# Three graph layers, regrouped: consecutive-node tiles, two column blocks, and an order written by hand

## The chip, the cores and the metric

The kernel runs on one core of a Trainium2 chip. The metric is the device time of one execution in microseconds (us); lower is better. The median of three runs before the change is 11253.15 us.

## The reference, cut to what matters

The graph has N = 3327 nodes with 128 features, and a dense-stored adjacency `adj` of 3327 x 3327 (fp32). Four layers each normalise `x`, apply a ReLU and add the layer's result to `x`:

```python
h = relu(layernorm(x)); x = x + L0(h, adj)   # 128 x 8-dim attention, softmax over N; ends in out @ Wo.T
h = relu(layernorm(x)); x = x + L1(h, adj)   # hyperbolic: h @ embed, scale per node, adj @ y, concat @ layer
h = relu(layernorm(x)); x = x + L2(h, adj)   # h @ weight.T, scale per node, adj @ xt, scale per node, relu
h = relu(layernorm(x)); x = x + L3(h, adj)   # (A/deg) @ h @ W_in + (A.T/deg_T) @ h @ W_out
```

The scalings per node of layers 1 and 2 are long chains on one number per node (norm, sqrt, tanh, artanh, division). So after layer 0 there are four products of an adjacency with a node matrix: `adj @ y` in layer 1, in layer 2, and in layer 3 once with `adj` and once with its transpose.

## The kernel before, in words

Layer 0 (lines 1 to about 800) is a hand-ordered attention that fills the first 10290 us; its instructions are the same, in the same order on every engine, before and after the change. It leaves its unnormalised heads in DRAM (`oT_d`, 8 rows and a row of sums) and a transposed adjacency `adjT`.

What follows runs in nine stretches, and a scheduler sets the order of their instructions:

- **Output projection** (loop at L876 to L891). For each pair of node tiles, `ot` is loaded from `oT_d` (1152 KB, L876), divided by its sums on DVE (`rc`, reciprocal, L878; product, L879), transposed on PE (L886), copied by ACT or DVE (`evac`, L132 and L136), multiplied with `woT` (L890) and added to `xs` (L891). A node tile `t` holds the nodes p*26+t, one per partition p.
- **Before product 1.** `layer_norm` (L922, L923, L927), transposes and sums of squares (`transposed_squares`, L957, L942, L946: squares on ACT, summed on PE with a vector of ones), a projection (`project`, L969) whose result DVE copies (L1044), sums of squares by rows (`row_squares`, L976, L977), and then the chain of small operations: class `Small` (L158 to L191) makes one 128 x 26 result per operation, on DVE, with `sqrt`, `tanh` and `Ln` on ACT (L185). Last, ACT and DVE write `y` (L1058, L981).
- **Product 1** (`aggregate`, L992 to L997). For each of 26 source tiles a strip of 128 rows x 3327 columns of `adjT` is loaded, from SP's and POOL's queue in turn, into one of four buffers. PE multiplies it with `y[:, t, :]` in seven column chunks of up to 494, which accumulate in seven PSUM banks. DVE sums each strip's rows (`degT`, L997) for layer 3.
- **Between products 1 and 2, 2 and 3**: the results leave PSUM through `by_tiles`, which reorders columns to the tiles, and the same kinds of steps follow for all 26 tiles at once.
- **Products 2, 3 and 4.** Product 3 reads `adj` itself, product 4 `adjT`; there is no work between 3 and 4 but the copies, and product 4 carries the projection of product 3's result beside it (`also`).
- **End.** `add_projected` (L1147) per four tiles, and stores of `out` from SP's and POOL's queue (L1166, L1169).

Nothing of a product starts before the steps in front of it are done for all nodes, since every product needs all of `y` as its sources. PE, DVE and ACT each run their instructions strictly in the order given.

Of the kernel before, what the change touches and what calls it, by code (L numbers as in the profile page):

```python
# [67 lines left out]
def rows_of(t):  # L68
    return P - 1 if t == NT - 1 else P
# [22 lines left out]
def gnn_kernel(ctx: ExitStack, tc: tile.TileContext, x, adj, Wq, Wk, Wv, Wo, embed, layer,  # L92
# [709 lines left out]

    wts = ctx.enter_context(tc.tile_pool(name="wts", bufs=1))
    xs = load_x(wts)
    ones = wts.tile([P, 1], F32, name="ones")
    nc.vector.memset(ones, 1.0)

    def on_all(v, name):
        o = wts.tile([P, D], F32, name=name)
        nc.sync.dma_start(o, v.unsqueeze(0).to_broadcast([P, D]))  # L810
        return o
# [15 lines left out]
    def clip_of(sm, n):  # L827

        return sm.ts(sm.recip(n), L2_MAXNORM, ALU.mult, 1.0, ALU.min)

    eb, lb, hb = on_all(embed_bias, "eb"), on_all(layer_bias, "lb"), on_all(bias, "hb")
    eb2, lb2, b2 = row_sum("eb2", eb), row_sum("lb2", lb), row_sum("b2", hb)
    with tc.tile_pool(name="w0", bufs=1) as w0:
        sm = Small(w0, "s")
        b2w = sm.new()
        nc.vector.tensor_copy(b2w, b2.to_broadcast([P, NT]))
        bn = sm.ts(sm.sqrt(b2w), L2_MIN_NORM, ALU.max)
        bt = sm.act(bn, AF.Tanh)
        bc = sm.mul(sm.div(bt, bn), clip_of(sm, sm.ts(bt, L2_MIN_NORM, ALU.max)))
        nc.vector.tensor_scalar(hb, hb, bc[:, 0:1], None, op0=ALU.mult)  # L840
    hb2 = row_sum("hb2", hb)
    emb_w = wts.tile([P, D + 1], F32, name="emb_w")
    nc.sync.dma_start(emb_w[:, 0:D], embed)
    lay_w = [wts.tile([P, D + 1], F32, name=f"lay_w{i}") for i in range(2)]
    for i in range(2):
        nc.sync.dma_start(lay_w[i][:, 0:D], layer[i * P:(i + 1) * P])
        with_product(lay_w[i], lb)
    with_product(emb_w, eb)
    w_in = wts.tile([P, D], F32, name="w_in")
    nc.sync.dma_start(w_in, W_in)  # L850
    w_out = wts.tile([P, D], F32, name="w_out")
    nc.sync.dma_start(w_out, W_out)
    w2T = wts.tile([P, D + 1], F32, name="w2T")

    degT = wts.tile([P, NT], F32, name="degT")
    nc.vector.memset(degT, 1.0)
    with tc.tile_pool(name="f1", bufs=1) as f1, tc.tile_pool(name="f2", bufs=4) as f2, \
            tc.tile_pool(name="f_ps", bufs=3, space=PSUM) as f_ps:
        w_raw = f1.tile([P, D], F32, name="w_raw")
        nc.sync.dma_start(w_raw, weight)  # L860
        ps = f_ps.tile([P, 4, P], F32, name="ps_t")
        nc.tensor.transpose(ps[:, 0, :], w_raw, ident)
        nc.vector.tensor_copy(w2T[:, 0:D], ps[:, 0, :])
        with_product(w2T, hb)
        wo = f1.tile([P, HD], F32, name="wo")
        nc.sync.dma_start(wo, Wo)
        wo_e = wo.rearrange("o (i e) -> o e i", e=H)
        woT = f1.tile([P, H, P], F32, name="woT")
        for k0 in (0, 4):
            ps = f_ps.tile([P, 4, P], F32, name="ps_t")  # L870
            for i in range(4):
                nc.tensor.transpose(ps[:, i, :], wo_e[:, k0 + i, :], ident)
            evac(woT[:, k0:k0 + 4, :], ps)
        for t0 in range(0, NT, 2):
            ot = f2.tile([P, H + 1, 2 * P], F32, name="ot")
            (nc.sync if t0 % 4 else nc.gpsimd).dma_start(ot, places(oT_d, t0, 2, H + 1))  # L876
            rc = f2.tile([P, 2 * P], F32, name="rc")
            nc.vector.reciprocal(rc, ot[:, H, :])  # L878
            nc.vector.tensor_tensor(ot[:, 0:H, :], ot[:, 0:H, :], rc.unsqueeze(1).to_broadcast([P, H, 2 * P]),  # L879
                                    op=ALU.mult)  # L880
            for i in range(2):
                oT = f2.tile([P, H, P], F32, name="oT")
                for k0 in (0, 4):
                    ps = f_ps.tile([P, 4, P], F32, name="ps_t")
                    for e in range(4):
                        nc.tensor.transpose(ps[:, e, :], ot[:, k0 + e, i * P:(i + 1) * P], ident)  # L886
                    evac(oT[:, k0:k0 + 4, :], ps)
                py = f_ps.tile([P, D], F32, name="ps_y")
                for e in range(H):
                    nc.tensor.matmul(py, oT[:, e, :], woT[:, e, :], start=(e == 0), stop=(e == H - 1))  # L890
                nc.vector.tensor_tensor(xs[:, t0 + i, :], xs[:, t0 + i, :], py, op=ALU.add)  # L891

    big = ctx.enter_context(tc.tile_pool(name="big", bufs=1))
    strips = ctx.enter_context(tc.tile_pool(name="strips", bufs=4))
    part = ctx.enter_context(tc.tile_pool(name="part", bufs=3))
    banks_u = ctx.enter_context(tc.tile_pool(name="banks_u", bufs=1, space=PSUM))  # L900

    def bank_u(i):
        return banks_u.tile([P, 4 * P], F32, name=f"pu{i}")

    turn = [0]

    def next_bank():
        turn[0] += 1
        return bank_u(turn[0] % 7)

    def arr(name, w=D):
        return big.tile([P, NT, w], F32, name=name)

    def matT(name):
        return big.tile([P, NP], F32, name=name)

    def layer_norm(sm, xs, h):

        mv = sm.pool.tile([P, NT, 2], F32, name="mv")
        for t in range(NT):  # L920
            st = part.tile([P, 6], F32, name="st", bufs=8)
            nc.vector.bn_stats(st, xs[:, t, :])  # L922
            nc.vector.bn_aggr(mv[:, t, :], st)  # L923
        r = sm.recip(sm.sqrt(sm.ts(mv[:, :, 1], LN_EPS, ALU.add)))
        off = sm.mul(sm.ts(mv[:, :, 0], -1.0, ALU.mult), r)
        for t in range(NT):
            nc.scalar.activation(h[:, t, :], xs[:, t, :], AF.Relu, scale=r[:, t:t + 1], bias=off[:, t:t + 1])  # L927

    def columns_of(c):
        ts = tiles_of(c)  # L930
        return slice(ts[0] * P, (ts[-1] + 1) * P)

    def column_squares(sm, of, dst_of=None):


        o = sm.new()
        ps = bank_u(7)
        for c in range(7):
            ts = tiles_of(c)
            src = of(c)  # L940
            sq = part.tile([P, 4 * P], F32, name="sq")
            nc.scalar.activation(sq[:, :len(ts) * P], src, AF.Square)  # L942
            if dst_of is not None:
                nc.vector.tensor_copy(dst_of(c), src)
            for t in ts:
                nc.tensor.matmul(ps[:, t:t + 1], sq[:, (t - ts[0]) * P:(t - ts[0] + 1) * P], ones,  # L946
                                 start=True, stop=True)
        nc.vector.tensor_copy(o, ps[:, :NT])
        return o

    def transposed_squares(sm, h, hT):

        def of(c):
            ps = next_bank()
            ts = tiles_of(c)
            for t in ts:
                nc.tensor.transpose(ps[:, (t - ts[0]) * P:(t - ts[0] + 1) * P], h[:, t, :], ident)  # L957
            return ps[:, :len(ts) * P]
        return column_squares(sm, of, lambda c: hT[:, columns_of(c)])

    def project(lhsT, w, take):

        k = w.shape[-1]
        step = 4 * P // k
        for t0 in range(0, NT, step):
            ts = range(t0, min(t0 + step, NT))
            ps = next_bank()
            for t in ts:
                nc.tensor.matmul(ps[:, (t - t0) * k:(t - t0 + 1) * k], lhsT[:, t * P:(t + 1) * P], w,  # L969
                                 start=True, stop=True)  # L970
            take(ts, ps[:, :len(ts) * k].rearrange("p (t o) -> p t o", o=k))

    def row_squares(dst, ts, rows):

        sq = part.tile([P, 4, P], F32, name="sq")
        nc.scalar.activation(sq[:, :len(ts), :], rows, AF.Square)  # L976
        nc.vector.tensor_reduce(dst[:, ts[0]:ts[-1] + 1], sq[:, :len(ts), :], axis=AX.X, op=ALU.add)  # L977

    def add_scaled(dst, a, s, b):

        nc.vector.scalar_tensor_tensor(dst, a, s, b, op0=ALU.mult, op1=ALU.add)  # L981

    def aggregate(y, strip_of, deg=None, also=None):


        width = [min(AW, N - c * AW) for c in range(7)]
        pu = [bank_u(c) for c in range(7)]
        for t in range(NT):
            m = rows_of(t)
            s = strips.tile([P, N], F32, name="strip")  # L990
            for p0, p1 in pieces(m):
                (nc.sync if t % 2 else nc.gpsimd).dma_start(s[p0:p1], strip_of(t, p0, p1))  # L992
# [208 lines left out]
```

## Time and profile before

| | us |
|---|---|
| median of three runs | 11253.15 |
| lowest, highest | 11250.1, 11254.57 |
| the profiled execution | 11256.11 |
| its span, first to last instruction | 11254.3 |
| the part behind layer 0 (from 10290.3) | 964.0 |

Busy shares over the whole span are PE 96%, ACT 90%, DVE 76%, but these are the shares of the attention. A row of the windows view gives the length of a stretch, then each engine's busy time with its number of instructions, then PE's granted clock as a fraction, the DMA engines' busy share and GB/s.

### The profile page before, as it was taken

To read this page: it belongs to the slowest core of one execution; us is meant where nothing else is said; L and a number is where in the kernel's file an instruction comes from. 1 tells how busy PE (TensorE), PEld (TensorE's weight loads), DVE (VectorE), ACT (ScalarE), POOL (GpSimd) and SP (SyncE) were. 2 spreads that over 40 slices of the span, in tenths; PEclk is the share of its full clock that TensorE was granted. 3 is DMA by queue.
4 is the path that set the end of the run, shared out by engine and by line. 5 is a ranking of instruction groups with operands and counts; after the bars stand their busy time and mean duration, and the time that the engine had idled before them with its cause. 6 is when DMAs were issued, how large, how long until landed. Compare 5 with 4: busy or idle time off the path is not lost. (4 is left out here: it accounts for less than half of the span.)

```text
span 11254.3 us, 205118 instructions
## 1 busy us (share of the span) xinstructions
PE 10750.9 (96%) x72980; PEld 3640.0 (32%) x72980; DVE 8537.9 (76%) x13563; ACT 10117.6 (90%) x13718; POOL 1974.8 (18%) x3079
## 2 busy tenths in 40 slices
PE   4599999999999999999999999999999999998779
PEld 2233333333333333333333333333333333334444
DVE  5588887888878887788887888878887777777533
ACT  3599999999999999999999999999999999996210
POOL 5111211111111111111111111111111111111000
PEclk8799999999999999999999999999999999999889
DMA  8855555555555554555555555555554545454457
GB/s 245 252 91 94 96 89 111 91 94 96 89 111 91 96 93 80 111 89 97 93 91 111 90 97 93 92 111 89 96 91 82 108 79 85 78 87 118 158 183 272
DMA packets 652680, 1243.35 MB, mean 110 GB/s; under 512 B 185966, under 2 KB 527990, under 8 KB 635148
## 3 DMA queue, kind: packets, MB, share of 16 engines
q1 hardware_dynamic: 609768, 1100.61, 50.4%
q0 software_dynamic: 41888, 129.51, 3.9%
q8 instruction: 591, 9.68, 0.4%
q14 instruction: 433, 3.55, 0.1%
HBM read 1082.90 MB, written 146.60 MB: 109 GB/s over the span
## 5 line engine op out<-in xcount | busy, mean ns | idle before, releaser
L659 ACT ACTIVATE e<-S 128x952 f32<-128x952 f32 (+1 forms) x9408 | 8697.9, 1146 | 14.5 <-PE S L647 11.4
L700 PE MATMUL po<-e,VA 128*9 128x476 f32 (+1 forms) x46592 | 5736.2, 564 | 20.2 <-DVE OS L708 1.1
L640 DVE TENSOR_TENSOR S<-a,shb 128x476 f32<-128x476 f32 (+1 forms) x5824 | 4037.5, 693 | 1760.9 <-ACT e L659 1299.5
L647 PE MATMUL S<-QS,KT 64*128 64x476 f32 (+1 forms) x23296 | 4843.4, 447 | 54.5 <-DVE S L640 45.8
L647 PEld LDWEIGHTS S<-QS,KT 64*128 64x128 f32 x23296 | 2410.3, 184 | 5143.4 <-ACT e L659 1465.8
L662 ACT ACTIVATE e<-S 128x476 f32<-128x476 f32 (+1 forms) x3808 | 2358.7, 758 | 2.4 <-PE S L647 2.1
L682 DVE SCALAR_TENSOR_TENSOR e<-e,h 128x476 f32<-128x476 f32 (+1 forms) x2016 | 1389.9, 689 | 46.2
L712 POOL DMA_DIRECT2D oT_d<-OS x896 | 470.7, 531 | 4791.2 <-DVE OS L708 4707.5
L566 POOL TENSOR_SCALAR QS<-QS 32x476 fp32r<-32x476 f32 (+1 forms) x1344 | 982.9, 731 | 1453.6 <-DMA QS<-qS_d 801.1
L700 PEld LDWEIGHTS po<-e,VA 128*9 128x9 f32 x46592 | 692.7, 88 | 1608.5 <-issue 1514.3
L673 DVE TENSOR_SCALAR h<-S 128x476 f32<-128x476 f32 (+1 forms) x672 | 439.0, 653 | 77.6 <-PE S L647 4.9
L677 DVE TENSOR_TENSOR h<-h,h 128x476 f32<-128x476 f32 (+1 forms) x672 | 443.1, 659 | 0.0
L684 DVE SCALAR_TENSOR_TENSOR e<-e,h 128x476 f32<-128x476 f32 (+1 forms) x672 | 440.8, 656 | 0.0
L682 DVE SCALAR_TENSOR_TENSOR e<-h 128x476 f32<-128x476 f32 (+1 forms) x672 | 438.3, 652 | 0.0
L576 POOL COPY VA<-VR 128x832 f32<-128x832 f32 x224 | 225.5, 1007 | 972.0 <-DMA VR<-v_d 733.8
L132 ACT COPY uT<-pu 128x494 f32<-128x494 f32 (+1 forms) x12 | 6.6, 547 | 428.2 <-PE pu L994 428.2
L675 DVE TENSOR_SCALAR h<-h 128x476 f32<-128x476 f32 (+1 forms) x672 | 323.4, 481 | 23.2
L994 PE MATMUL pu<-strip,h 128*128 128x494 f32 (+2 forms) x728 | 294.6, 566 | 38.9 <-ACT h L927 38.9
L994 PE MATMUL pu<-strip,y 128*128 128x494 f32 (+2 forms) x728 | 296.5, 570 | 29.3 <-DVE y L981 18.3
L679 DVE TENSOR_SCALAR h<-h 128x476 int32<-128x476 f32 (+1 forms) x672 | 279.3, 416 | 23.0
L291 DVE STREAM_TRANSPOSE cols<-rows 128x416 f32<-128x416 f32 x208 | 204.1, 986 | 21.8 <-DMA rows<-in_adj_dram 14.2
L994 PEld LDWEIGHTS pu<-strip,h 128*128 128x128 f32 (+1 forms) x728 | 138.5, 191 | 191.2 <-issue 141.8
(184 smaller groups left out, 2319.0 us busy)
## 6 DMA issues: line engine op xcount, KB each, us to landing
KT<-kS_d SPq DMA_DIRECT2D x1792, 208.0 KB
KT<-kS_d SPq DMA_DIRECT2D x1792, 104.0 KB
VR<-v_d SPq DMA_DIRECT2D x224, 416.0 KB
strip<-adjT POOLq DMA_DIRECT2D x39, 1663.5 KB, 7.7
strip<-adjT SPq DMA_DIRECT2D x36, 1663.5 KB
QS<-qS_d SPq DMA_DIRECT2D x3072, 14.9 KB
QS<-qS_d SPq DMA_DIRECT2D x1536, 29.8 KB
adjT<-cols SPq DMA_DIRECT2D x26, 1664.0 KB
```

What stands on the lines that cost most here:

```text
L566: nc.gpsimd.tensor_scalar(QS[b][r0:r0 + 32, j + 1, :w], QS[b][r0:r0 + 32, j, :w].bitcast(F32), -1.0, 0.0, op0=ALU.mult, op1=ALU.add)
L640: touch(u, [r], nc.vector.tensor_tensor(bank(u, r), adj_of[c][2 * q + r][:, :w], shift_of[c][:, :w], op=ALU.subtract))
L647: x = nc.tensor.matmul(bank(u, r), KT[b][64 * r:64 * r + 64, max(0, j - 1), q * P:(q + 1) * P], QS[b][64 * r:64 * r + 64, j, :w], start=Fa ...
L659: touch(u, (0, 1), nc.scalar.activation(e[:, :, :w], S[:, odd:even + 1, :w], AF.Exp, scale=2.0))
L662: touch(u, [r], nc.scalar.activation(e[:, 1 - r, :w], bank(u, r), AF.Exp, scale=2.0))
L673: touch(u, [1], nc.vector.tensor_scalar(f, bank(u, 1), LOG2_E2, EXP_LEAST, op0=ALU.mult, op1=ALU.max))
L677: nc.vector.tensor_tensor(f, f, whole, op=ALU.subtract)
L682: nc.vector.scalar_tensor_tensor(e, f if k == 4 else e, EXP_C[k], f, op0=ALU.add, op1=ALU.mult)
L684: nc.vector.scalar_tensor_tensor(e, e, EXP_C[0], power.bitcast(F32), op0=ALU.add, op1=ALU.mult)
L700: nc.tensor.matmul(po[32 * j:32 * j + H + 1, :w], VA[k % 2][:, 2 * pairs[v][2] + of, j, :], e_of[v, j][:, 1 - of, :w], start=(q == 0 and r ...
L712: nc.gpsimd.dma_start(oT_d[:, d * N + c * CW:d * N + c * CW + w], o[32 * j:32 * j + H + 1, :w])
L994: nc.tensor.matmul(pu[c][:, :w], y[:m, t, :], s[:m, c * AW:c * AW + w], start=(t == 0), stop=(t == NT - 1))
```

## The change

Everything behind layer 0 is rewritten; what is computed stays the same. The parts:

- A node tile now holds 128 consecutive nodes. `x`, `out`, `oT_d` and the strips are read and written in that layout: 512-byte runs for `x`, `out` and `oT_d`, consecutive rows for the strips. Results leave PSUM in plain column order (`copied`), without `by_tiles`.
- The 26 tiles are two blocks, `BLOCKS = (range(0, 16), range(16, 26))`. Each product is made in two column blocks of 2048 and 1279 columns (four and three PSUM banks of up to 512 columns); product 4 in three, of 1791, 1024 and 512. A strip is one block's columns of 128 rows: 234 strips instead of 104, in six buffers.
- The steps before and behind a product run per block, as Python generators (`pre1`, `post1`, `pre2`, `post2`, `pre3`), each step followed by a `yield` of the us that it is taken to last. `aggregate` calls `tick` after every matmul, which issues the next steps when their time has come; `drain` issues all that is left. A scheduler no longer moves anything (`manual_schedule`).
- The second block's `y` is waited for only at source tile 16 (`drain(ready)`).
- The projection of layer 0 goes tile by tile, with loads four tiles ahead (`f_load`, `f_norm`, `f_turn`, `f_mul`), and block 0's `pre1` starts beside its last ten tiles.
- Squares of `h` are summed by rows on ACT and DVE (`squared`), no longer on PE; the degrees are summed per block (four `deg` vectors).

```diff
+    BLOCKS = (range(0, 16), range(16, NT))
-    strips = ctx.enter_context(tc.tile_pool(name="strips", bufs=4))
+    strips = ctx.enter_context(tc.tile_pool(name="strips", bufs=6))
+    ctx.enter_context(tc.manual_schedule())
...
+    def tick(us):
+        while chains and us > 0:
+            c = chains[0]
+            if c[1] > us:
+                c[1] -= us
+                return
+            us -= c[1]
+            try:
+                c[1] = next(c[0])
+            except StopIteration:
+                chains.popleft()
+
+    def drain(until=None):
+        while chains and (until is None or until in chains):
+            for _ in chains.popleft()[0]:
+                pass
...
+    def feed(k):
+        while strip_list and len(strip_held) < k:
+            rows, t, c0, w = strip_list.popleft()
+            s = strips.tile([P, 4 * 4 * P], F32, name="strip")
+            for p0, p1 in pieces(rows_of(t)):
+                (nc.sync if t % 2 else nc.gpsimd).dma_start(s[p0:p1, :w], rows[t * P + p0:t * P + p1, c0:c0 + w])
+            strip_held.append(s)
...
+        for t in range(NT):
+            if ready is not None and t == second[0]:
+                drain(ready)
+            feed(6)
+            m = rows_of(t)
+            s = strip_held.popleft()
+            for c in cs:
+                k = width(c)
+                nc.tensor.matmul(got[c][:, :k], y[:m, t, :], s[:m, c * 4 * P - c0:c * 4 * P - c0 + k],
+                                 start=(t == 0), stop=(t == NT - 1))
+                tick(k * 0.00172)
+            if deg is not None:
+                nc.vector.tensor_reduce(deg[:m, t:t + 1], s[:m, :deg_w or w], axis=AX.X, op=ALU.add)
...
+    use(7, 4, 5, 6)
+    ready = start(pre1(1))
+    start(keep1(0))
+    start(keep1(1))
+    got = aggregate(ys[0], first, 0, ready=ready, deg=deg[0], deg_w=final[0][0] * P)
+    drain()
+    use(7, 0, 1, 2, 3)
+    start(both(post1, pre2, 0, got))
+    got = aggregate(ys[0], second, 4)
+    drain()
+    use(7, 4, 5, 6)
+    ready = start(both(post1, pre2, 1, got))
+    got = aggregate(ys[1], first, 0, ready=ready)
+    use(7, 0, 1, 2, 3)
+    start(both(post2, pre3, 0, got))
+    got = aggregate(ys[1], second, 4)
+    drain()
```

`keep1` is the projection with the first half of `layer`; `use` names the PSUM banks left to the steps; `both` runs one block's `post` and the next layer's `pre`.

## The prediction

> **What bounds the kernel now.** I read the stretches behind layer 0 first (windows view): the change leaves the first 10290 us instruction for instruction as they are.
>
> ```profile
> 10290.30:10330.00 39.70, 2.46 (x10) 1.79 (x10) 20.42 (x38) 3.60 (x5) 5.25 (x8) 0.54 0.98 324
> 10330.00:10413.50 83.50, 76.50 (x624) 72.30 (x624) 76.20 (x124) 16.50 (x27) 5.04 (x5) 0.96 0.46 147
> 10413.50:10472.30 58.80, 37.75 (x183) 31.66 (x183) 32.64 (x126) 28.14 (x62) 0.00 (x0) 0.64 0.00 1
> 10472.30:10621.00 148.70, 148.00 (x364) 69.89 (x364) 89.01 (x51) 8.99 (x28) 6.94 (x13) 0.98 0.80 286
> 10621.00:10730.90 109.90, 49.40 (x235) 43.17 (x235) 67.09 (x315) 44.12 (x85) 0.00 (x0) 0.56 0.05 18
> 10730.90:10880.00 149.10, 148.41 (x364) 70.04 (x364) 9.41 (x29) 9.02 (x28) 6.86 (x13) 0.98 0.80 286
> 10880.00:10939.60 59.60, 14.31 (x78) 13.99 (x78) 45.28 (x158) 16.23 (x27) 0.00 (x0) 0.56 0.08 29
> 10939.60:11239.00 299.40, 299.21 (x780) 144.86 (x780) 92.08 (x60) 13.63 (x33) 12.69 (x24) 0.99 0.76 273
> 11239.00:11254.30 15.30, 6.07 (x52) 5.88 (x52) 7.01 (x27) 0.30 (x1) 7.14 (x14) 0.82 0.36 113
> ```
>
> Columns: stretch, length, then busy us of PE, PEld, DVE, ACT, POOL, then clock, DMA share, GB/s. The four products (rows 4, 6, 8) are PE-bound. Between them lie 58.8 + 109.9 + 59.6 = 228.3 us in which no product runs, and 123.2 us of projection. PE's waits say what is late there:
>
> ```profile
> PE pu L957 <- ACT h L927: 48.4, 2, 40.3
> PE pu L994 <- ACT h L927: 38.9, 1, 38.9
> PE ps_t L862 <- DMA ot<-oT_d: 34.7, 1, 34.7
> PE pu L994 <- DVE y L981: 18.3, 1, 18.3
> PE ps_t L886 <- ACT oT L132: 4.5, 13, 0.7
> ```
>
> The reader is to see the per-node chains on DVE and ACT, and a first load. The price of a product comes from two finer windows:
>
> ```profile
> 10472.30:10476.30 4.00, 4.00 (x5) 1.79 (x6) 0.50 0.00 0
> 10476.30:10480.30 4.00, 4.00 (x10) 1.82 (x9) 0.86 0.00 0
> 10500.00:10600.00 100.00, 100.00 (x252) 47.54 (x251) 1.00 0.84 305
> ```
>
> At full clock, 252 half-products in 100 us at 475 columns on average: 1.67 ns a column, 144.5 us for 26 x 3327. A start after an idle PE runs at clock 0.50 and 0.86 first: about 3 us lost.
>
> **The change part by part.** Block pieces of a product cost 26 x columns x 1.67 ns: 88.9 us (2048), 55.5 (1279), 77.8 (1791), 44.5 (1024), 22.2 (512). PE work of the steps now lies beside them at the full-clock price of its rows: 0.27 us a tile for a 129-wide projection (L969), 0.24 for a sum with ones (L946), 0.17 for a transpose (L957). Counts are from the changed kernel's own order of instructions.
>
> *Projection of layer 0* (123.2 us now). In front of tile 2's load SP issues Wo, tile 0 and all of `x`; POOL issues two tiles and nine small loads. That is 5.1 MB, at the first row's 324 GB/s 16 us, so tile 2 is there at about 10310. Then 24 tiles at 2.9 us (before: 5.8 us from one pair's L890 to the next), 6 us for the last tile's division, transposes and products: 10386. DVE has 0.87 + 1.14 + 0.27 = 2.3 us of its own a tile (half of L878 and L879, and L891) and gets some 19 us of preparation and layer norm in bursts, of which its 0.6 us a tile hide a part; I take 14: 10400, or 110 us. The loads are 30,000 packets of 512 bytes. Such packets moved at 289 GB/s (the loads of Wq and Wk at 11 to 13 us), so 17 MB take 59 us and the first strips 14 more, under PE's pace; if latency uncovers them it costs up to 20. Bounds 98 to 133.
>
> *Before product 1* (58.8 now): layer norm's statistics and ReLU lie under the last tiles. What is left for block 0: 4.6 us of ReLU and squares, 23 small operations 9 (with `Ln`'s table), first copies 1, six projections 6.5 at ACT's 1.04 us a group (copy and square 0.5 each), then 52 small operations, which take 11.9 us now (10460.4 to 10472.3): 34.
>
> *Product 1, first piece.* 88.9 + PE work 11.4 + a cold start 3. DVE issues in order: `y` of block 0 (5 us), statistics, degree sums of 1.65 us (L997's 3.62 for 3327 columns, by width), 23 small operations, so the first copy of `hT` is done near 28 us and the third near 31, while PE comes to the projection at 23: 10 us of stall with the ReLU before it. The 52 operations in one burst hold up the degree sums and with them the strips' buffers: strip 11 lands near 58 us, wanted at 53: 4.5. Together 118.
>
> *Product 1, second piece, with `post1` and `pre2` of block 0.* PE needs 55.5 + 8. The chain: sums and projection 26 us (paced by PE), 46 small operations 12, `xs` 32 x 0.263 = 8.4, statistics 4.2, small 3.4, ReLU 16 x 0.39 = 6.2, squares 2.5, small 8.5, copies and projection 8.5, and 60 small 14.7 (10716.2 to 10730.9 now): 94.5. Uncovered: 95.5 - 63.5 = 32.
>
> *Product 2, first piece.* The same chain with 10 tiles in front of source tile 16: PE first waits 4 us for ACT's squares behind block 0's `y`; then 19 to the end of the projection, 12, 5.3, 2.6, 3.4, 3.9, 2, 8.5, PE's projection at 64 to 69, and 60 small operations and a first `y`, 15.5: `y` of tile 16 at about 86 us. PE is there at 70. Then 34.2 and a cold start 3: 123.
>
> *Other pieces.* `post2` and `pre3` of block 0 need 43 us and have 62.5 (55.5 + 6.5 and a copy): hidden. For block 1 they need 52 and have 60: hidden, 88.9 + 4 + 2 = 95. Their cover gone, they would cost those 43 and 52. Then 55.5, 78, 54.5 (44.5 and 40 tiles of 0.22, L1147, under 1.2 us a group), 26 (with 2 for loads of 256 KB each, for which PE takes 0.85 us).
>
> *End* (15.3 now): one four-tile group instead of seven, one store instead of 21 issues: 9.
>
> *Strips:* 243 issues instead of 108 at POOL's 0.53 us, alternately on two queues, against 0.85 us or more of PE time each; the rate needed is the same or lower (250 GB/s over these pieces, now 305). Nothing.
>
> *Waits.* PE gets some 69 groups of step work between its products, each behind ACT or DVE. Where such a result just arrives, PE waited 4.5/13 = 0.35 us. Bounds 0 and 24; most have slack by the prices above, so 6. Behind each such wait stand the rest of the piece on PE, then the strips' buffers, and on SP and POOL the loads of the next strips; nothing else is queued there until the stores of the end.
>
> Sum: 110 + 34 + 118 + 95.5 + 123 + 62.5 + 95 + 55.5 + 78 + 54.5 + 26 + 9 + 6 = 867, now 964.0: 97 us less. The span 11254.3 becomes 11157.3; the median of the runs lies 1.15 below this span: **11156**.
>
> Splitting doubles the per-node chains: 583 small operations and 50 table loads instead of 301 and 24. A table load takes 1.283 us in the trace, and the `sqrt` behind it starts 0.02 us later (10319.23 behind 10317.93 + 1.28), with 0.14 us between DVE's result and the load. The Trainium skill ("ScalarE: Activation LUTs", What ACT_TABLE_LOAD costs) counts a further drain of about 1.38 us for each switch, 2.66 in all. By the row the sum stands; with the page's drain on the 29 loads of the uncovered chains an estimate would be 40 us more, 11196. The trace shows no such drain, so it stays out of the sum.
>
> **The rivals.** *A, the guesses of the order are short, PE waits often* (14%). For: the `yield` of a ReLU is 0.28 us against the row's 0.39, and bursts are counted at 0.3 or 0.5 of their length. Against: most steps end on DVE and ACT, which run ahead of PE. All 69 waits at 0.35 (+18) and four stalls of 5 us with a cold start of 3 (+32): 11206.
>
> *B, more is hidden* (14%). For: DVE is 40% idle in product 1 and nearly free in product 2; my chains add stages end to end. If a third of 32 + 16 + 14.5 + 34 is gone: -32, 11124.
>
> *C, the cover fails: slower* (4%). One engine order; if the chains of the blocks ran with the products stopped, as PE's waits on `y` would do if the order were wrong, all per-block chains would be paid: 34 + 60 + 94.5 + 85 + 43 + 52 = 368 against the 110 that I leave uncovered (34 + 17.5 + 32 + 19 + some 7): 258 more, 11414. It decides for slower from 97 us, that is when less than 161 of the 258 us are covered. Against: the operands of the first piece's sources 0 to 15 do not depend on block 1.
>
> *D, the change does not do what it says* (2%): if the first piece waited for all 26 tiles of `y` and not for block 0, the gaps would stay as they are; projection and end save 13 + 6: 11234.
>
> *E, a table switch costs about twice its row* (2%): another 1.283 us on each of the 29 switches of the uncovered chains is 37: 11193. Against: the 0.02 and 0.14 us above. (The Trainium skill's drain, cited there, is of this size.)
>
> **How the numbers follow.** My forecast 65%, A 14%, B 13%, C 4%, D 2%, E 2%. Its own range, from the projection (-12, +23), the waits (-6, +18) and 15 us either way in the two long chains: 11128 to 11190. To leave out no more than 2 in 10 with B and A: 11118 to 11210. A measurement of this kernel tells 0.2% (22 us) from no change. Faster by more: my forecast, A, B and E, 94%; within: D, 2%; slower: C, 4%.
>
> **What would show it.** In the profile of the changed kernel: product pieces at clock 1.00 and 1.67 ns a column; PE waiting on DVE `y` once before product 2 (about 25 us) and once in its first piece (about 16); in product 1's first piece stalls on the copy of `hT` and on a strip; none in layer 3; end of the projection near 10400. I am wrong if PE waits on strips all along, if layer 2 to 3 shows a gap, or if the projection takes over 133 us.

## The result, and the profile after

| | before | after |
|---|---|---|
| median of the runs, us | 11252.85 (11250.1 to 11254.57, 4 runs) | **11114.46** (11112.16 to 11115.49, 4 runs) |
| span of the profiled execution | 11254.3 | 11113.3 |
| end of layer 0 (its last product on PE) | 10290.2 | 10284.7 |
| the part behind it | 964.1 | 828.6 |

The ratio is 0.9877, with a 95% interval of 0.986 to 0.9894: 138.4 us less. The prediction said 97 less, 11156, in a range from 11118 to 11210; the time lies 3.5 us below that range. The direction was right; the predicted saving was 41 us too small.

Windows view of the changed kernel, one row per stage of the prediction's sum (stretch, length, busy us of PE, PEld, DVE, ACT, POOL, clock, DMA share, GB/s):

```profile
10284.70:10398.20 113.50, 83.28 (x639) 80.28 (x636) 75.31 (x152) 38.08 (x69) 21.30 (x29) 0.85 0.69 208
10398.20:10429.50 31.30, 9.01 (x48) 7.27 (x47) 20.93 (x92) 18.44 (x39) 0.63 (x2) 0.70 0.09 34
10429.50:10531.20 101.70, 101.19 (x291) 49.51 (x292) 72.33 (x164) 30.54 (x71) 6.87 (x13) 0.98 0.67 237
10531.20:10594.30 63.10, 63.10 (x223) 36.87 (x222) 35.39 (x152) 24.53 (x45) 6.87 (x13) 1.00 0.82 269
10594.30:10621.70 27.40, 7.90 (x49) 7.50 (x47) 20.20 (x96) 13.22 (x27) 0.00 (x0) 0.63 0.29 121
10621.70:10737.00 115.30, 100.97 (x278) 48.59 (x279) 50.19 (x234) 39.62 (x83) 6.87 (x13) 0.92 0.63 209
10737.00:10798.10 61.10, 61.10 (x205) 34.77 (x204) 24.55 (x107) 23.64 (x43) 6.87 (x13) 1.00 0.82 275
10798.10:10891.10 93.00, 92.89 (x240) 42.55 (x239) 76.99 (x116) 18.53 (x35) 6.87 (x13) 1.00 0.80 296
10891.10:10946.90 55.80, 55.80 (x157) 29.63 (x156) 35.25 (x25) 1.40 (x3) 6.87 (x13) 1.00 0.89 302
10946.90:11025.00 78.10, 78.10 (x209) 39.50 (x208) 52.14 (x37) 2.00 (x5) 6.87 (x13) 1.00 0.86 299
11025.00:11078.70 53.70, 53.70 (x186) 28.80 (x186) 11.36 (x40) 1.25 (x3) 8.03 (x15) 1.00 0.80 247
11078.70:11105.80 27.10, 25.75 (x69) 10.88 (x67) 2.25 (x8) 0.58 (x1) 5.36 (x10) 1.00 0.74 232
11105.80:11113.30 7.50, 1.16 (x8) 0.97 (x8) 1.12 (x4) 0.58 (x1) 0.00 (x0) 0.79 0.13 37
```

Rows 3, 4 and 6 to 12 are product pieces; in them PE is busy all the time, but for 14.3 us of row 6 (115.30 less 100.97), 1.4 of row 12, 0.5 of row 3 and 0.1 of row 8. Of the three stretches before products 1, 2 and 3, once 228.3 us, there remain row 2 (31.3) and row 5 (27.4); the third is gone. PE's waits behind layer 0 (who waited for whom, us in total, times, longest):

```profile
PE pu L1035 <- issue: 29.2, 2, 15.3
PE pu L1035 <- DVE y L912: 14.2, 1, 14.2
PE pu L961 <- DVE hT L942: 12.8, 3, 8.1
...
PE pu L1035 <- DMA strip<-adjT: 1.2, 3, 0.5
PE pu L1290 <- ACT uT L987: 0.7, 1, 0.7
```

The first row is the two starts, before product 1 (13.9) and before product 2 (15.3). The view names no releaser there ("issue"), but both starts stand 0.45 us behind the first of DVE's writes of `y` (10429.07 and 10621.23; PE 10429.53 and 10621.68). The second row is the wait for `y` of source tile 16 in product 2. Of the third, 8.1 and 4.2 lie in front of products 1 and 2, so only 0.5 us in a product. Stage by stage against the prediction:

| stage | predicted | measured | off |
|---|---|---|---|
| projection and the steps before product 1 | 144 | 144.8 | +0.8 |
| product 1, first piece | 118 | 101.7 | -16.3 |
| second piece with the gap behind it | 95.5 | 90.5 | -5.0 |
| product 2, first piece | 123 | 115.3 | -7.7 |
| product 2 second, product 3 | 213 | 209.9 | -3.1 |
| product 4 | 158.5 | 158.9 | +0.4 |
| end | 9 | 7.5 | -1.5 |
| waits, as a term of its own | 6 | in the rows above | -6.0 |
| layer 0 | as before | 5.5 shorter | -5.5 |

Together 44 us: the span came out at 11113.3, where the sum gave 11157.3. (By medians it is 41, since the median lies 1.2 us above the profiled span here and 1.45 below it in the kernel before.) Three questions remain for experiments: whether layer 0's 5.5 us belong to the change, whether it is the cover that saves the time, and why the estimated stalls did not come.

### The profile page after: what moved, and what is told of

The parts are those of the page before. It is cut to its first block, busy times and chain, and to the rows that moved or that the text cites. A ratio compares the mean times of both kernels' runs of the same rounds, so it can differ in the third digit from the quotient of the medians.

```text
span 11113.3 us, 205604 instructions
## 1 busy us (share of the span) xinstructions
PE 10706.3 (96%) x72876; PEld 3602.0 (32%) x72876; DVE 8565.0 (77%) x13863; ACT 10187.7 (92%) x13845; POOL 2014.2 (18%) x3149
## 5 line engine op out<-in xcount | busy, mean ns | idle before, releaser
L659 ACT ACTIVATE e<-S 128x952 f32<-128x952 f32 (+1 forms) x9408 | 8702.4, 1150 | 13.0 <-PE S L647 10.4
L1035 PE MATMUL pu<-strip,y 128*128 128x512 f32 (+2 forms) x1456 | 600.6, 567 | 44.8 <-issue 29.2
L1035 PEld LDWEIGHTS pu<-strip,y 128*128 128x128 f32 (+1 forms) x1456 | 272.9, 192 | 322.4 <-issue 288.5
L1039 DVE TENSOR_REDUCE deg<-strip 128x1 f32<-128x1536 f32 (+3 forms) x104 | 192.8, 1881 | 77.7 <-DMA strip<-in_adj_dram 41.0
```

The source lines that it names most:

```text
L659: touch(u, (0, 1), nc.scalar.activation(e[:, :, :w], S[:, odd:even + 1, :w], AF.Exp, scale=2.0))
L1035: nc.tensor.matmul(got[c][:, :k], y[:m, t, :], s[:m, c * 4 * P - c0:c * 4 * P - c0 + k], start=(t == 0), stop=(t == NT - 1))
```

## The experiments

The part behind layer 0 ("the tail", 828.6 us in the changed kernel) is given beside the medians, since it is free of what layer 0 does. The kernel before had medians from 11246.97 to 11252.33 in the sets of runs made beside the variants, so some 5 us between medians of different sets need no edit. Each variant has one profile, and the tail of the kernel before was 964.1 and 961.9 in its two, so tails less than some 2 us apart are not told apart.

**Layer 0.** The kernel before, profiled again.

> The kernel before, profiled a second time; it asks whether layer 0, the same instructions in both kernels, took 5.4 us less in the changed kernel's profile (10284.7 against 10290.2) because of the change. Theory 'drift': the end of layer 0 moves by some us from one profiled execution to the next, so it may stand anywhere between 10284 and 10292 here, and the rest of the span stays at 964 within 2 us. Rival 'the change shortens layer 0': it ends at 10290 again, within 1 us, and every variant of the changed kernel ends it near 10285.

It ended layer 0 at 10286.3, with a tail of 961.9 (964.1 in the first profile). The variants below, whose layer 0 is the same code, ended it anywhere from 10283.4 to 10292.0. The 5.5 us are drift between executions, no part of the change.

**No cover.** In front of each `aggregate` of products 1 to 3 that has steps beside it (and no `ready` any more), as here:

```diff
     start(both(post1, pre2, 0, got))
+    drain()
     got = aggregate(ys[0], second, 4)
```

> The changed kernel with all steps of a block emitted before the product piece beside which they run, in layers 1 to 3 (the same work, no cover). Theory 'the cover carries the saving': each block's chain is paid in full, less the step work that no longer lies inside the pieces: about 34 us more in the first piece of product 1, 46 at the second, 39 in the first piece of product 2, 40 in the second, 32 in the first of product 3, together some 190: 11305 (11270 to 11372; the prediction's rival with no cover said 258 more, 11372), slower than the kernel before. Rival 'the saving is less work, not cover': under 60 us more, below 11175.

Measured 11226.67 (11222.14 to 11231.88, 10 runs), 0.9981 of the kernel before (0.9971 to 0.999); tail 942.4. So this cover is worth 113.8 of the 135.5 us by which the tail shrank, and the rest of the change (projection, end, layout, less what doubling the chains costs) the other 22. Some cover is left in this run: block 0's first steps still lie beside the projection, and what DVE and ACT do behind PE's last step of a chain still runs beside the product. Without its cover the kernel is not slower than the one before, as both theories with full payment had it (11305, 11372): both prices (190 and 258 us) were too high for this order, the prediction's 258 by more than a factor of two. Windows view of this kernel: steps before product 1, its first piece, steps, second piece, steps, first piece of product 2.

```profile
10401.10:10479.70 78.60, 25.77 (x131) 21.71 (x130) 55.26 (x233) 46.12 (x104) 0.63 (x2) 0.63 0.04 14
10479.70:10569.20 89.50, 89.46 (x210) 39.36 (x209) 39.69 (x23) 2.41 (x5) 6.87 (x13) 1.00 0.78 270
10569.20:10636.90 67.70, 21.29 (x112) 17.75 (x113) 43.82 (x182) 29.54 (x56) 0.00 (x0) 0.60 0.03 12
10636.90:10692.90 56.00, 56.00 (x158) 29.48 (x157) 16.00 (x79) 13.07 (x31) 6.87 (x13) 1.00 0.83 286
10692.90:10743.60 50.70, 14.35 (x71) 11.91 (x71) 32.30 (x147) 23.09 (x44) 0.00 (x0) 0.58 0.16 68
10743.60:10833.80 90.20, 90.16 (x210) 39.64 (x208) 13.22 (x73) 11.82 (x26) 6.87 (x13) 0.99 0.78 268
```

Three things are read here. The pieces alone take 89.5 and 56.0 us, so the price of 1.67 ns a column was right. The steps of block 0 between the pieces take 67.7 us alone, where beside the second piece they took 90.5: beside the product, where PE's steps of the chain take their turn between the matmuls, that chain is 23 us longer. And `post2` and `pre3` hardly show up as stops: the products paused for only 9.5 us before the second piece of product 2 and 6.3 before the first of product 3, and PE was at work on the chains' own steps for all but 1.2 and 1.1 of it. One more stop, 5.8 us, lies inside that first piece of product 3, on a strip. POOL could issue its load only when DVE came to the degree sums, behind the chain:

```profile
PE pu L1035 <- DMA strip<-in_adj_dram: 5.8, 1, 5.8
10928.85 0.53 POOL L1014 DMA_DIRECT2D strip<-in_adj_dram  x1 [30.55 <-DVE deg L1039]
```

So the chains held up a product in three ways here: through PE's few steps in them, through the `y` that the product reads, and through strip buffers that wait for DVE. The rest ran on DVE and ACT beside the product, in this order too.

**Function tables.** `Part.act` calls `AF.Copy` instead of its function, so the square roots, logarithms and hyperbolic tangents are left out.

> The changed kernel with the square roots, logarithms and hyperbolic tangents of the small operations behind layer 0 replaced by plain scaled copies, so that no function table is switched there (another result is computed; the same number of instructions otherwise). Theory 'loads run ahead of their operands': only the eight loads that stand in the chain of waits cost anything, 8 x 1.28 = 10 us less: 11104 (11098 to 11108). Rival 'every load of the uncovered chains is paid': 29 x 1.28 = 37 less, 11077. Rival 'and each again as much as a drain' (the Trainium skill, ScalarE: Activation LUTs, What ACT_TABLE_LOAD costs): 77 less, 11037.

11112.56 (11108.22 to 11116.42): 1.9 less; tail 826.3, 2.3 less, hardly more than two profiles of one kernel differ by. Even the eight loads that stand in the chain of waits cost about a fifth of their 10 us, if that. ACT's timeline in the changed kernel (start, us, instruction, idle before it and its releaser) says why:

```profile
10433.44 1.28 ACT L185 ACT_TABLE_LOAD   x1
10439.89 0.21 ACT L185 ACTIVATE p<-p 128x10 f32<-128x10 f32 x1 [5.17 <-DVE p L170]
...
10462.12 1.28 ACT L185 ACT_TABLE_LOAD   x1
10465.88 0.21 ACT L185 ACTIVATE p<-p 128x10 f32<-128x10 f32 x1 [2.48 <-DVE p L170]
```

The load stands ahead of the wait: it starts as soon as ACT is free, and is over 5.17 and 2.48 us before the operand comes from DVE. Where ACT comes to the load late, it delays the chain: the load at 10607.52 left DVE idle for 0.92 us, where it waits 0.28 for such a result otherwise.

**Strips.** Four buffers instead of six.

> The changed kernel with four buffers for strips instead of six. The prediction put 4.5 us of stall on a strip in the first piece of product 1, because 52 small operations hold up VectorE's degree sums and with them the strips' buffers; the changed kernel showed none. Theory 'the hold-up is there, and six buffers cover it': they hold 6 x 3.41 = 20.5 us of TensorE's work, four hold 13.6; a load lands 6.7 us after its issue, so a sum that comes more than 7 us behind its products stalls TensorE: 4 to 12 us more in that piece alone, 11118 to 11127. Rival 'there is no hold-up': that piece stays at 101.6 us and the kernel at 11114.

11147.09 (11144.55 to 11152.3), 33 slower; the first piece of product 1 takes 111.6 us, 10 more. Its one stop there, in PE's waits, behind which PE ran at a clock of 0.50 again:

```profile
PE pu L1035 <- DMA strip<-adjT: 7.2, 1, 7.2
```

It was the eleventh strip, there 48.4 us after the start and wanted at 41.2; POOL issued its load 2.2 us behind the end of the 52 operations, behind the first degree sum after them. The hold-up of the buffers behind DVE is real; six buffers cover it. That the whole kernel lost more than that piece I had not expected. One strip in product 3 cost 6.4 us, again one whose load waited for DVE's degree sums (20.95 us). But the last two pieces, which have no such sums, took 3.6 and 6.5 us more too: narrow strips need the depth also where nothing holds up DVE.

**The uncovered chains.** Four edits, each alone and then together. First, squares and transposes beside the ReLU of the same four tiles:

```diff
-        for t in ts:
-            nc.scalar.activation(h[:, t, :], xs[:, t, :], AF.Relu, scale=sm.at(r, t), bias=sm.at(off, t))
-            yield 0.28
+        for four in fours(ts):
+            for t in four:
+                nc.scalar.activation(h[:, t, :], xs[:, t, :], AF.Relu, scale=sm.at(r, t), bias=sm.at(off, t))
+                yield 0.35
...
+                row_squares(sm, o, four, nodes(h, four))
+                yield 0.5
+                turned(h)(four)
+                yield 0.5
```

> The changed kernel with squares, transposes and copies of hT emitted beside the ReLU of the same four tiles, ahead of the 23 small operations, instead of behind them. Theory 'the uncovered chains set the time': 5 us less before product 1, 5 less in the 27.4 us between products 1 and 2, 3 less of the 14.2 us for which TensorE waits for y of tile 16: 13 less, 11101. Rival 'VectorE and ScalarE are the limit there, the order is all the same': within 3 us of 11114. Rival 'TensorE then waits for the ReLU inside the pieces': 5 us or more slower, 11119 and up.

11106.74 (11106.15 to 11111.14), 7.7 less, of the 13 expected; tail 6.6 less. Before product 1: 26.6 instead of 31.3; the gap before product 2: 23.6 instead of 27.4. The wait for `y` of tile 16 stayed, 13.3: something else sets it. The next edit asked what. `post1(1)`'s copies, squares and sums go beside `pre2(0)`, and PE comes earlier to block 1's later steps:

```diff
+            yield from received_early(*beside)
...
         yield from project(sm, hT, w2T, take_a(sm, aa))
+        if beside:
+            summed_early(beside[0])
...
-        yield cost()
+        yield cost() * (0.3 if b else 1.0)
```

> The changed kernel with the first steps of block 1 behind product 1 (three copies of uT, their squares, the sums with ones) put beside block 0's last steps in the 27.4 us before product 2, and block 1's later steps there reached by TensorE after 10 products fewer. Theory 'the wait for y of tile 16 comes from where TensorE's order puts block 1's steps': the 14.2 us and the cold start of 2.7 behind it go, 2.5 of sums move under the gap, which grows by 1 to 2: 17 less, 11097 (11093 to 11101). Rival 'block 0's chain pays for it': the gap grows by 5 or more, 11104 or above. Rival 'the chain itself takes those 80 us': no change, 11114.

11104.57 (11104.25 to 11110.32), 9.9 less. The wait is gone and the first piece of product 2 takes 103.8 us instead of 115.3; the gap before it stays, 27.6. In the changed kernel block 1's ReLU was over at 10669.5 and PE came to its transposes at 10674.9, so PE's place in the order had a part in this wait; the edit also starts block 1's chain earlier, and no run parts the two. Of the 17 us expected, the tail gained 7.9: 2.9 came back as a wait of PE for block 1's ReLU, which it now reaches too early, the projection of layer 0 happened to take 3.4 more in this execution, in the same instructions, and some 3 are not accounted for. Third, the adds in `post1` a group ahead of the sums of squares, and the sums with ones closer together:

```diff
-            row_squares(sm, ww, ts, nodes(w1, ts)[:, :, 0:D])
+            late.append(ts)
+            if len(late) > 1:
+                row_squares(sm, ww, late[-2], nodes(w1, late[-2])[:, :, 0:D])
...
-            yield 1.2
+            yield 0.4
```

> The changed kernel with VectorE's adds of the next three tiles standing ahead of the sums of squares of the last three in post1 (now VectorE idles 0.67 us in each group for ScalarE's square), and the sums with ones 0.4 instead of 1.2 us of product apart. Theory 'the chain of block 0 behind product 1 sets the start of product 2': 4 + 3 = 7 us less of the 27.4, 11107 (11104 to 11110). Rival 'that chain has slack there': within 2 us of 11114.

11108.74 (11108.4 to 11116.13), 5.7 less; tail 4.8 less. The gap shrank as expected, 20.5 instead of 27.4, but the first piece of product 2 took 117.8, 2.5 more: PE came to block 1's transposes 55.6 us after its start, in the changed kernel 53.2. Fourth, `load_nodes()` behind the loads of tiles 2 and 3.

> The changed kernel with the loads of attention tiles 2 and 3 issued ahead of x. Theory 'tile 2 is late because SyncE issues x first' (VectorE idles 7.2 us for that load at 10309): 5 us less in the projection, 11109 (11106 to 11111). Rival 'bytes': the same 5.1 MB are in front of the third tile's end either way, so within 2 us of 11114; slower by up to 3 if the first sum with x waits.

11114.67 (11110.73 to 11120.61): nothing; tail 0.4 less. DVE waited 18.0 us for the first three tiles instead of 19.0, so the order of the loads does not set that; the bytes in front may.

**Together.**

> The four edits together (steps turned early, front of block 1 early, skewed sums, attention tiles loaded first). If they are independent as the theories say: 8 (measured for the first alone) + 17 + 7 + 5 = 37 less than the changed kernel, 11077 (11070 to 11092). If the chains of the two blocks only trade places, 11095 or above.

11097.89 (11097.35 to 11107.28), 16.6 less, not the 37 that the theories together had. The tail, 808.9, is 19.7 less, and the four tails alone sum to 19.7 too (6.6 + 7.9 + 4.8 + 0.4), but the stages do not add: the second piece with its gap took 89.0, where the first and third edit alone had brought it to 87.6 and 84.1. The trace shows PE at block 0's last transposes at 10590.8, when their ReLU and squares had ended at 10585.0, and ACT copying block 1's results at 10594.6, ahead of block 0's projection. A second version mended both places.

> A second version of the four edits, without the load order: block 1's copies and squares stand behind block 0's hyperbolic tangent before product 2 (in the first version ScalarE held block 0's copies of the projection behind them until product 1 had ended), and TensorE reaches block 0's transposes some 6 us earlier (in the first version it came 5 to 7 us after their ReLU). Theory: the gap before product 2, 24.6 us there, shrinks to 13, all else as there: 11086 (11080 to 11092). Rival 'TensorE then waits for the ReLU inside the second piece, and gains nothing': 11095 or above.

11102.38 (11099.67 to 11105.43), tail 811.7: no gain, where 11086 was expected. The gap did shrink, to 16.9, but the second piece took 70.2 us instead of the changed kernel's 63.1, since it now holds block 0's transposes and projection. And PE was granted half its clock for 6.8 us in it, 3.4 us lost, from the end of the 32 sums with ones on. Windows of PE before and in that stretch (stretch, length, PE, clock, DMA share, GB/s):

```profile
10537.00:10540.00 3.00, 3.00 (x21) 1.00 0.77 246
10541.00:10547.00 6.00, 6.00 (x14) 0.50 0.36 109
```

In the second pieces of products 1 and 2 and in the first of product 3, such stretches of 3.4 or 6.8 us at 0.50 follow six of the twelve groups of these sums in the four variants that issue them closer together (none in the third edit alone, one in the first version, three here, two in the last variant), and none of the three in the changed kernel. Why some groups and not others is open. They cost this variant some 6.8 us and the first version 1.7, so what the second version is worth by itself is not settled. Last, the same with `pre1(0)` under the projection of layer 0:

```diff
-        if t == first[-1]:
+        if t == 12:
             drain()
             start(pre1(0))
-        tick(1.1)
+        tick(1.1 if t < 12 else 2.0 if t < NT - 10 else 3.0)
```

> The same with block 0's first steps started at node tile 12 of the projection and given 2 to 3 us of it per tile instead of 1.1, so that they lie beside its last ten tiles. Theory 'they hide where TensorE has half its time idle': 10 us (5 to 18) of the 26.6 before product 1 go: 11076 (11068 to 11081). Rival 'VectorE, busy 73 of these 107 us, is the limit': the projection takes longer by what the steps gain, within 4 us of the run before.

**11094.5** (11091.27 to 11096.13), ratio to the kernel before 0.9859 (0.9843 to 0.9876): the fastest here, 20 us below the changed kernel, with a tail of 805.9. The intervals of the two ratios overlap; the tails, 22.7 us apart, do not depend on layer 0. Windows view of projection and steps before product 1 together, in this kernel:

```profile
10288.50:10427.50 139.00, 93.45 (x682) 89.31 (x682) 95.78 (x245) 58.06 (x113) 21.68 (x31) 0.83 0.56 170
```

In the second version of the four edits, without this one:

```profile
10292.00:10433.10 141.10, 92.15 (x681) 87.06 (x681) 95.79 (x244) 56.66 (x107) 21.93 (x31) 0.83 0.58 175
```

And in the changed kernel:

```profile
10284.70:10429.50 144.80, 92.30 (x685) 87.55 (x682) 96.24 (x244) 56.52 (x107) 21.93 (x31) 0.82 0.56 170
```

The 26.6 us of steps vanished behind the projection, and the projection grew by 24: 2.1 us gained, not the 10 expected. That is what the rival had said; its reason is not shown, since DVE has 96 us of work in these 139 and PE 93, and neither is full. I take it that their waits for each other fill the rest; no run tried which. The rest of the 5.8 us of tail against the second version is about the 3.4 us of clock that were lost there and not here.

## Why the prediction was right, and where it was wrong

**Right:** what bounds the kernel (the no-cover run), the price per column (89.5 and 56.0 alone, for 88.9 and 55.5), layer 3 with 1.5 us of stops in all, and the two places where PE would still wait for `y`. Partly luck: projection plus first steps (144.8 for 144) is 113.5 for 110 and 31.3 for 34, two errors that cancel; so is the wait inside product 2 (14.2 for 16), since both its ends came early, by 6.5 and 4.8 us. None of the prediction's three signs of being wrong appeared; all of them looked for a slower kernel.

**Product 1, first piece: the term that failed most, 118 for 101.7.** The 88.9, the PE work (9.2 by the trace, for 11.4) and the cold start (32 half-products in 16.38 us, 0.427 each when warm, so 2.7, for 3) were right or near; of the 14.5 us of stalls there came 0.5. This is the step that failed: DVE's bursts of small operations were taken as longer than they are, and so the stalls of PE behind them. Two places. *"23 small operations 9 ... so the first copy of `hT` is done near 28 us"*: I had taken 9 us from the kernel before, where DVE has copies and sums of the projection in between; there the 23 stretch over 11.8 us:

```profile
10446.28 0.17 DVE L170 TENSOR_SCALAR s<-s 128x26 f32<-128x26 f32 x1
10446.36 0.55 DVE L1044 COPY a<-pu 128x387 f32<-128x387 f32 x1
...
10453.01 0.56 DVE L1044 COPY a<-pu 128x387 f32<-128x387 f32 x1
10453.48 0.18 DVE L191 SCALAR_TENSOR_TENSOR s<-s,s 128x26 f32<-128x26 f32 x1
```

DVE's timeline in the changed kernel:

```profile
10447.43 0.17 DVE L170 TENSOR_SCALAR p<-p 128x10 f32<-128x10 f32 x1
...
10451.82 0.17 DVE L158 TENSOR_TENSOR p<-p,p 128x10 f32<-128x10 f32 x1
10451.91 0.68 DVE L942 COPY hT<-pu 128x512 f32<-128x512 f32 x1
```

4.5 us for the 23, and the copy is there 23 us after the start, not 28, when PE arrives: 0.48 us of wait. *"The 52 operations ... hold up the degree sums and with them the strips' buffers: strip 11 lands near 58 us"*: the mechanism was right, as the run with four buffers shows (7.2 us), but the burst came and went earlier. It was over 41 us after the start (10470.5), and the load that it held up was issued at 43.2; with 6.7 us from issue to landing, the prediction's 58 would put that near 51. By the same 6.7, an estimate, the strip was there at 50, and PE came to it, the thirteenth, at 51.3: six buffers were enough by little more than 1 us.

**Second piece and gap, 95.5 for 90.5; first piece of product 2, 123 for 115.3.** The same kind of term again: 4.7 for 8.5 at the 23 operations, 12.8 for 14.7 at the 60. Longer than predicted were the 32 updates of `xs` (10.4 for 8.4) and the statistics (6.3 for 4.2). In product 2 `y` of tile 16 came 79.5 us after the start instead of 86, and PE was there at 65.2 instead of 70. What I had not seen is that the place of block 1's steps in the order has a part in these 79.5: putting their front ahead and PE's steps forward, together, took the wait away. (The terms of the chain of 94.5 sum to 94.4; what the last 1 us of the 95.5 is, the sum does not say.)

**Waits, 6 for nothing.** The 69 groups of PE's steps cost 0.5 us in product 1 and 0.7 in product 4. Where it was looked at, the order's guesses were late rather than early (5.4 us between block 1's ReLU and PE's transposes in product 2), which costs nothing on PE at once, but can show up as the wait for tile 16.

**The rivals.** B (more is hidden) named the right direction: of its 96.5 us (32 + 16 + 14.5 + 34) 23 were gone, 14 of them the stalls. The stalls went because the bursts are short; that DVE's idle time did it, as B had it, is not shown. (It stands with 14% in one place of the prediction and 13% in the other; the chances sum to 100 with 13.) Its 11124 lies 10 above the result, about the drift, the waits and the rest together. C's 258 fell: 113.8 in all, because `post2` and `pre3` (95 of the 368) made the products pause for 15.8 us, most of it PE's own work, and for 5.8 more by a late strip, and the other chains are shorter alone (67.7 for the 94.5). E fell with the table run. The Trainium skill ("ScalarE: Activation LUTs", What ACT_TABLE_LOAD costs) counts 2.66 us with the drain for each switch. By that figure an estimate for the 29 is 77 us; taking all of them out brought 2, so the measurement does not agree with it here. D did not occur: PE started each first piece with block 0 alone.

**The range** ended 3.5 us too high since nearly all the errors had one sign: the bursts of 23 and 60 small operations were priced too high, the first from rows with other work in between, and the projection's and the waits' bounds were drawn as if independent of that. That the time fell outside is in part bad luck: without the 5.5 us of layer 0's drift between the two profiled executions it would be near 11120, 2 us inside the range. The 14 us of stalls that did not come are a fault of the mechanism's timing either way.

## What to carry to other kernels

Price a burst of dependent small operations from a stretch where nothing else stands in that engine's stream, and look whether table loads stand ahead of the wait. A chain beside a product stops it where TensorE takes part in it, where the product reads the chain's result, and where a buffer of the product waits for the engine that the chain occupies: count those places, and check for each whether TensorE comes before or after the data. Savings of single edits do not add up where one stream fills the gaps of another: test them together, and compare the stage, not the whole time, where an unchanged part drifts by more than the edit is worth.

## What the hardware showed that was not expected

- A table load does not wait for the operand of the function behind it (1.28 us, over 5.17 and 2.48 us ahead of it).
- The same layer 0 ended between 10283.4 and 10292.0 us in thirteen profiled executions; 8.6 us is more than most of the single edits are worth.
- PE's granted clock fell to 0.50 for 6.8 us in a stretch in which PE was never idle, at the end of 32 products of one column each (second piece of product 1, second version of the four edits); in the last variant the same stretch ran at 1.00. With these products closer together such a fall followed six groups of twelve, in the changed kernel none of three.
